# Linear attention followed by four Mamba scales: a tile of its own for inputs times step sizes, kept small weights, folded weights reloaded, attention weights for two passes

## The chip, the cores and the metric

The kernel runs on one core of one Trainium2 chip. The time is device microseconds of one execution; lower is better. The core has five engines with an instruction queue each: PE (matrix multiply, with its weight loads PEld), DVE (vector), ACT (activation functions), POOL (GpSimd) and SP, which here issues every DMA. Engines wait for each other by semaphores.

## What is computed

The input x has 8 samples of 512 channels and 48 x 48 = 2304 positions. Two layers follow each other; each adds its result to its input after a group norm:

```python
x = x + attention(gn(x))          # 8 heads of 64, causal, linear, feature elu+1
x = x + mamba4(gn(x))             # four scales of 128 channels, each fed by the one before

# one scale (b samples, L = 2304 positions, 128 channels in, 256 inside, 16 states)
xz = u @ Wi.T;  xp, z = split(xz, 2)
xs = silu(conv1d(xp, wc, 4 taps, depthwise, causal) + bc)
dt, Bm, Cm = split(xs @ Wx.T)                     # 8, 16, 16
delta = softplus(dt @ Wdt.T + bdt)
h_t = exp(delta_t * A) * h_(t-1) + (delta_t * xs_t) * B_t     # A = -exp(A_log)
y_t = (h_t . C_t) + xs_t * D
x_m = (y * silu(z)) @ Wo.T
fused = max(x_i, x_m)
out_i = sigmoid(mean(x_i)) * x_i + sigmoid(mean(fused)) * fused
x_(i+1) = split_(i+1) + out_i
```

All is float32.

## The kernel before

Positions are cut into 6 chunks of 384 columns. **Attention** works through 32 passes (8 samples x 4 tiles of 128 output channels), 6 chunks each: `chunk(m)`, lines 273 to 496. Its projections (L293) read the weights from `wq_sb`, which holds all 1536 output columns; `load_projections` (L106) loads the columns of one tile with three DMAs, and all four tiles are loaded in the start-up. In the first pass of a sample POOL also normalises the input xn (L317) and it is stored for the other three passes.

**Mamba** runs as two streams of four samples each. A stream takes a sample through its four scales; one sample and scale is a block, of six chunks. A chunk of a block is a job: 8 slots of two of the 16 states times two halves of the 256 channels, with four scans a slot. The 192 jobs of both streams alternate by a fixed list (`turns`, after four jobs of stream 0 alone). In each slot POOL and DVE form the products of B and delta times xs in `u` (L856, L867), ACT forms the decays in PSUM banks (L877), DVE runs the four scans (L888), POOL multiplies the result by C (L900), and PE sums it into `yp` (L916). `u` has five buffers, PSUM six banks.

**What orders the work.** The program is written out by hand: each slot has two halves, and preparations are tasks (generators) that stop at each `yield` with a time (in halves) and a number of banks; `beside` (L1056) advances those that are due. Each engine executes its instructions in the order in which the program writes them, SP its DMAs too. A task runs up to its first `yield` when it is made (L980).

**The parts that the change touches.**

- `Job.prepare` (L681) prepares one job: convolution (L693) and gate (L704) matmuls, silu, the projection to B, C and dt (L740), the step sizes delta = softplus (L764, into the one buffer of the tile delta), then `spread` (L771): delta is stored in a scratch in DRAM (L773, dscr) and read back spread over the partitions as dr. POOL multiplies delta by xs in place (L805), and the same tile is stored again (L773, xscr) and read back as dxr. Spreading is held to one job at a time by the list `spreading`.
- In the last job of a block, just ahead of the first `spread`, L769 makes the task `Stream.weights` (L510) for the stream's next block. It issues nine loads: in-projection wi, convolution wk (one row broadcast over the partitions), wo, wx, wd in two parts, pv in two parts, av. ACT then forms -exp of av (L536, L540), and POOL multiplies each of the four taps of wk by the projection (L539), so that the convolution becomes four matmuls on the raw input. `scaled` tells the next block's first job that wk is ready. This happens 32 times.
- `Stream.pass_on` (L561) ends a block and gives the stream its next input: ACT scales (L654, L655, L665), POOL adds (L662, L667, L670).
- `statistics(b)` (L216) forms the group norm of a sample for attention. For sample 0 it is the start-up: the six chunks of x, the weights of the first attention tile, the first xn, then the other tiles' weights.

## Time and profile before

| | |
|---|---|
| median of three runs | 8714.22 us (8709.94 to 8722.78) |
| the profiled execution | 8723.09 us |
| its span, first to last instruction | 8721.0 us |
| mean granted PE clock | 0.964 |
| DMA bytes of the program's own queue | 1635.13 MB |

| line | engine and work | count | mean ns |
|---|---|---|---|
| L888 | DVE scan | 6144 | 938 |
| L867 | DVE product | 1536 | 1195 |
| L900 | POOL weighing by C | 1536 | 3185 |
| L856 | POOL product | 1536 | 1283 |
| L805 | POOL delta times xs | 384 | 1005 |
| L539 | POOL folding of wk | 128 | 743 |
| L317 | POOL normalising xn | 192 | 673 |
| L877 | ACT decay | 6144 | 578 |

How to read it: a row of the profile names line, engine, operation and tiles (out<-in), how often it ran, its busy time and mean length, and the idle time of its engine just before it with what ended that idle time. Busy is not the same as on the path: only waits that delay the engine that is late at that place lengthen the run.

### The profile page before, as it was taken

The page shows a single profiled execution, that of the slowest core. Times are in us where ns is not written, and L with a number is a line of the kernel's source. Part 1 is how long each engine was busy: PE and PEld are TensorE (multiplying, and loading weights), DVE is VectorE, ACT ScalarE, POOL GpSimd, SP SyncE. Part 2 cuts the span into 40 slices and gives each one's busy share as a digit, 9 for nine tenths or more (in the row PEclk, how much of TensorE's full clock was granted, in tenths as well). Part 3 has the DMA queues.
Part 4 walks back from the last instruction along what each step waited for, and adds up shares of the span by engine and source line. Part 5 has one row for each costly group of instructions (what it writes and reads, how often), then busy time and mean ns, then how long its engine had stood idle before and what let it go on. Part 6 is the DMA issues. An engine that isn't in the chain of part 4 may idle for free. (4 is left out here: it accounts for less than half of the span.)

```text
span 8721.0 us, 124881 instructions
## 1 busy us (share of the span) xinstructions
PE 7774.7 (89%) x36482; PEld 3714.5 (43%) x36482; DVE 8072.2 (93%) x11078; ACT 6852.0 (79%) x14500; POOL 7834.3 (90%) x4343
## 2 busy tenths in 40 slices
PE   7899999988899999998889999999889999999965
PEld 4444444444444444444444444444444444444422
DVE  2899999999899999998899999999889999999998
ACT  2788888777788888877778888887777888888876
POOL 1789999999999999998998999998999889999998
PEclk9999999999999999999999999999999999999987
DMA  5667777776766777776676777776666667766665
GB/s 183 168 178 190 196 198 197 191 191 189 195 188 190 193 200 199 197 189 191 187 193 186 193 190 197 196 197 187 188 185 194 188 188 190 189 188 185 183 165 146
DMA packets 1002924, 1643.11 MB, mean 188 GB/s; under 512 B 138592, under 2 KB 797312, under 8 KB 1002240
## 3 DMA queue, kind: packets, MB, share of 16 engines
q1 hardware_dynamic: 1002240, 1635.13, 69.1%
q8 instruction: 290, 4.75, 0.2%
q14 instruction: 394, 3.23, 0.1%
HBM read 1309.06 MB, written 325.58 MB: 187 GB/s over the span
## 5 line engine op out<-in xcount | busy, mean ns | idle before, releaser
L888 DVE TENSOR_TENSOR_SCAN u<-bank,u 128x385 f32<-128x385 f32 (+1 forms) x6144 | 5455.4, 938 | 327.4 <-ACT bank L877 288.3
L900 POOL TENSOR_TENSOR u<-u,C 128x1536 f32<-128x1536 f32 x1536 | 4892.7, 3185 | 345.6 <-DVE u L888 186.9
L877 ACT ACTIVATE bank<-dr,av 128x385 f32<-128x385 f32 (+1 forms) x6144 | 3405.1, 578 | 671.0 <-DVE u L888 575.2
L916 PE MATMUL yp<-u,cst 128*64 128x384 f32 x12288 | 2417.7, 515 | 343.9 <-POOL u L900 259.6
L856 POOL TENSOR_TENSOR u<-B,dxr 128x512 f32<-128x512 f32 x1536 | 1969.9, 1283 | 17.5 <-DMA dxr<-xscr 15.4
L867 DVE TENSOR_TENSOR u<-B,dxp 128x1024 f32<-128x1024 f32 x1536 | 1835.0, 1195 | 9.7 <-ACT dxp L840 9.7
L293 PE MATMUL bank<-xn,wq_sb 128*128 128x384 f32 x4608 | 1725.8, 519 | 74.2 <-DVE u L888 33.0
L916 PEld LDWEIGHTS yp<-u,cst 128*64 128x64 f32 x12288 | 780.7, 139 | 1557.9 <-issue 871.9
L693 PE MATMUL bank<-xi,wk 128*128 128x384 f32 x3072 | 1110.7, 505 | 198.6 <-ACT kl L390 108.7
L293 PEld LDWEIGHTS bank<-xn,wq_sb 128*128 128x128 f32 x4608 | 867.4, 199 | 842.4 <-DVE u L888 140.0
L693 PEld LDWEIGHTS bank<-xi,wk 128*128 128x128 f32 x3072 | 558.8, 192 | 761.4 <-ACT kl L390 211.6
L805 POOL TENSOR_TENSOR delta<-delta,xs 128x384 f32<-128x384 f32 x384 | 385.7, 1005 | 361.8 <-DMA dscr<-delta 234.6
L305 ACT ACTIVATE ex<-bank,bqkv_sb 128x384 f32<-128x384 f32 x384 | 221.5, 577 | 505.3 <-PE bank L293 505.3
L877 ACT ACT_TABLE_LOAD x382 | 490.1, 1283 | 6.8
L845 ACT ACTIVATE yp<-xs,pv 128x384 f32<-128x384 f32 x384 | 223.6, 582 | 278.0 <-DVE yz L928 277.5
L934 PE MATMUL bank<-yz,wo 128*128 128x384 f32 x768 | 302.1, 510 | 24.4 <-DVE yz L928 17.3
L753 PE MATMUL bank<-dbc,wd 9*128 9x384 f32 x768 | 312.4, 527 | 3.7 <-ACT dbc L745 3.7
L704 PE MATMUL bank<-xi,wi 128*128 128x384 f32 x768 | 287.5, 495 | 9.7 <-ACT xs L729 9.7
L423 PE MATMUL bank<-cst,rdb 128*128 128x128 f32 x576 | 110.0, 304 | 200.9 <-DVE u L888 198.7
L740 PE MATMUL bank<-xs,wx 128*40 128x384 f32 x768 | 280.0, 487 | 2.7 <-ACT sm L457 2.7
L476 PE MATMUL bank<-sm,v 128*64 128x128 f32 x2304 | 257.1, 302 | 0.0
L729 ACT ACT_TABLE_LOAD x192 | 246.3, 1283 | 3.6 <-PE bank L693 0.2
(117 smaller groups left out, 7978.0 us busy)
## 6 DMA issues: line engine op xcount, KB each, us to landing
B<-scr SPq DMA_DIRECT2D x1536, 192.0 KB
C<-scr SPq DMA_DIRECT2D x1536, 192.0 KB
xn<-xn SPq DMA_DIRECT2D x192, 768.0 KB
dr<-dscr SPq DMA_DIRECT2D x768, 192.0 KB
dxr<-xscr SPq DMA_DIRECT2D x768, 192.0 KB
dscr<-delta SPq DMA_DIRECT2D x192, 384.0 KB
xscr<-delta SPq DMA_DIRECT2D x192, 384.0 KB
xn<-in_x SPq DMA_DIRECT2D x48, 768.0 KB
```

Of the source, the lines that this page charges most:

```text
L293: nc.tensor.matmul(ps, wq_sb[:, kt, j * 512 + o * P : j * 512 + (o + 1) * P], xn[:, kt, :], start=(kt == 0), stop=(kt == 3),)
L693: nc.tensor.matmul(xc, wk[:, k, h * P : (h + 1) * P], xi[:, c0 + k : c0 + k + LC], start=(k == 0), stop=(k == 3),)
L704: nc.tensor.matmul(zp, wi[:, 256 + h * P : 256 + (h + 1) * P], xi[:, c0 + 3 : c0 + 3 + LC], start=True, stop=True,)
L753: nc.tensor.matmul(vp, wd[32:41, h * P : (h + 1) * P], dbc[32:41, :], start=True, stop=True)
L805: nc.gpsimd.tensor_tensor(delta[:, h, :], delta[:, h, :], xs[:, h, :], ALU.mult)
L856: nc.gpsimd.tensor_tensor(u[:, :, :, 1 + LC - TAIL :], self.B[s % 4][:, :, cols].unsqueeze(2).to_broadcast(shape), self.dxr[s // 4][:, :, ...
L867: nc.vector.tensor_mul(u[:, :, :, 1 : 1 + LC - TAIL], self.B[s % 4][:, :, cols].unsqueeze(2).to_broadcast(shape), self.dxp.unsqueeze(1).to ...
L877: nc.scalar.activation(dA[:, cols], self.dr[h][:, g, cols], AF.Exp, scale=self.w[6][:, 2 * h + g, q + j : q + j + 1],)
L888: nc.vector.tensor_tensor_scan(u[:, j, g, cols], dA[:, cols], u[:, j, g, cols], 0.0, ALU.mult, ALU.add,)
L900: nc.gpsimd.tensor_tensor(u[:, :, :, 0:LC], u[:, :, :, 1:], self.C[s % 4].unsqueeze(2).to_broadcast([P, NG, 2, LC]), ALU.mult,)
L916: nc.tensor.matmul(self.yp[g * 64 : g * 64 + 64, 0:LC], pair_sum, u[:, j, g, 0:LC], start=False, stop=(s % 4 == 3 and j == NG - 1), skip_g ...
L934: nc.tensor.matmul(self.xm[:, 0:LC], self.w[2][:, h, :], self.yz[:, h, :], start=(h == 0), stop=(h == 1),)
```

## The change

There are four edits. (1) Delta times xs is written into a tile `dx` with one buffer; `spread` takes the tile to store. (2) Gate, out-projection, x-projection, bias, D and A of all four scales are packed into one array and loaded once into `scales`, step weights with their bias into `steps_w`; ACT forms -exp of A once for all scales, after the start-up's statistics. Uses index these tiles by the scale s. (3) `weights` loads only wk and, while a scale hasn't been folded, the projection wi: the folded wk is stored in DRAM once a scale, and later blocks of that scale, of either stream, load it back with one DMA. The list `folding` lets one stream fold at a time. (4) Attention weights are held for two passes: the tile wq of one pass (768 KB, packed on the host in one contiguous piece) has two buffers, and is loaded by one DMA in the fifth chunk of the pass before, right after that chunk has issued its fetch of the next xn.

```diff
-    wq_sb = cpool.tile([P, 4, 1536], F32, name="wq_sb")
-    def load_projections(o):
-        src = wqkv.rearrange("(t p) c -> p t c", p=P)
-        for j in range(3):
-            cols = slice(j * 512 + o * P, j * 512 + (o + 1) * P)
-            nc.sync.dma_start(out=wq_sb[:, :, cols], in_=src[:, :, cols])
+    wqs = []
+    def load_projections():
+        i = len(wqs)
+        if i < 4 * B:
+            o = parts[i * NC][1]
+            w = apool.tile([P, 4, 3 * P], F32, tag="wq", name=f"wq_{i}", bufs=2)
+            nc.sync.dma_start(out=w.rearrange("p t c -> p (t c)"), in_=wqkv[o])
+            wqs.append(w)
+    scales = cpool.tile([P, 4, 628], F32, name="scales")
+    steps_w = cpool.tile([64, 4, 256], F32, name="steps_w")
+    w_gate, w_out = scales[:, :, 0:256], scales[:, :, 256:512].rearrange("p s (h d) -> p s h d", h=2)
+    w_x = scales[:, :, 512:592].rearrange("p s (h d) -> p s h d", h=2)
+    w_cols = scales[:, :, 592:596]
+    w_a = scales[:, :, 596:628].rearrange("p s (h d) -> p s h d", h=4)
+    def load_scales():
+        nc.sync.dma_start(out=scales, in_=wall)
+        nc.sync.dma_start(out=steps_w[32:41], in_=wdt)
+        nc.scalar.activation(w_a, w_a, AF.Exp)
+        nc.scalar.mul(w_a, w_a, -1.0)
...
# chunk(m)
-                    wq_sb[:, kt, j * 512 + o * P : j * 512 + (o + 1) * P],
+                    wqs[m // NC][:, kt, j * P : (j + 1) * P],
...
         fetch(m + 1)
+        if c == NC - 2:
+            load_projections()
...
# Stream.weights: the nine loads, L536, L539 and L540 before; now
+            wk = wpool.tile([P, 4, 256], F32, tag=f"wk{z}", name=f"wk_{n}")
+            flat = wk.rearrange("p k d -> p (k d)")
+            self.coming = wk, s
+            if s in folded:
+                nc.sync.dma_start(out=flat, in_=folded[s])
+            else:
+                while folding:
+                    yield "1w", 0
+                folding.append(n)
+                wi = wpool.tile([P, 256], F32, tag="wi", name=f"wi_{n}")
+                nc.sync.dma_start(out=wi, in_=win[s])
+                nc.sync.dma_start(out=flat, in_=wconv[s].to_broadcast([P, 1024]))
+                for k in range(4):
+                    yield "3", 0
+                    nc.gpsimd.tensor_tensor(wk[:, k, :], wk[:, k, :], wi, ALU.mult)
+                folding.clear()
+                if s not in folded:
+                    folded[s] = dpool.tile([P, 1024], F32, tag="folded", name=f"folded_{s}")
+                    save(folded[s], flat)
             self.scaled = True
...
# Job.prepare
-            def spread(what):
-                s = dpool.tile([256, LC], F32, tag="dscr", name=f"{what}_{n}", bufs=6)
-                nc.sync.dma_start(out=s.rearrange("(h p) l -> p h l", h=2), in_=delta)
-                return s.rearrange("(h g d) l -> h d g l", h=2, g=2)
-            dsrc = spread("dscr")
+            def spread(what, of):
+                to = dpool.tile([256, LC], F32, tag="dscr", name=f"{what}_{n}", bufs=6)
+                nc.sync.dma_start(out=to.rearrange("(h p) l -> p h l", h=2), in_=of)
+                return to.rearrange("(h g d) l -> h d g l", h=2, g=2)
+            dsrc = spread("dscr", delta)
...
+            dx = mpool.tile([P, 2, LC], F32, tag="dx", name=f"dx_{n}", bufs=1)
             for h in range(2):
                 yield "1", 0
-                nc.gpsimd.tensor_tensor(delta[:, h, :], delta[:, h, :], xs[:, h, :], ALU.mult)
+                nc.gpsimd.tensor_tensor(dx[:, h, :], delta[:, h, :], xs[:, h, :], ALU.mult)
             yield "2", 0
-            xsrc = spread("xscr")
+            xsrc = spread("xscr", dx)
...
# start
         Task(statistics(0)).finish()
+        load_scales()
```

In `statistics(0)` the one remaining `load_projections()` loads the first pass's weights; the loop that loaded the other three tiles is gone. The other uses (gate, bias, x-projection, step weights, D, decay scale, out-projection) read the kept tiles in place of wi, pv, wx, wd, av and wo.

More of the change, by code (lines that the diff above doesn't have):

```diff
@@ L59, in attention_then_mamba_kernel @@
     wconv: bass.AP,
-    bconv: bass.AP,
-    wxp: bass.AP,
+    wall: bass.AP,
     wdt: bass.AP,
-    bdt: bass.AP,
-    alog: bass.AP,
-    dskip: bass.AP,
-    wout: bass.AP,
     out: bass.AP,
@@ L230, in statistics @@
                 load(c)
-            load_projections(0)
+            load_projections()
             for c in range(NC):
@@ L237, in statistics @@
                     fetch(0)
-            for o in range(1, 4):
-                load_projections(o)
         else:
@@ L340, in chunk @@
         fetch(m + 1)
+        if c == NC - 2:
+            load_projections()
         if o:
@@ L496, in chunk @@
             done[b, o] = norm
+    folded, folding = {}, []
     class Stream:
@@ L514, in weights @@
             self.scaled = False
-            wi = wpool.tile([P, 512], F32, tag=f"wi{z}", name=f"wi_{n}")
-            nc.sync.dma_start(out=wi, in_=win[s])
             wk = wpool.tile([P, 4, 256], F32, tag=f"wk{z}", name=f"wk_{n}")
-            nc.sync.dma_start(
-                out=wk.rearrange("p k d -> p (k d)"), in_=wconv[s].to_broadcast([P, 1024])
-            )
-            wo = wpool.tile([P, 2, P], F32, tag=f"wo{z}", name=f"wo_{n}", bufs=2)
-            nc.sync.dma_start(out=wo, in_=wout[s])
@@ L524, in weights @@
-            wx = wpool.tile([P, 2, 40], F32, tag=f"wx{z}", name=f"wx_{n}")
-            nc.sync.dma_start(out=wx, in_=wxp[s])
-            wd = wpool.tile([64, 256], F32, tag=f"wd{z}", name=f"wd_{n}")
-            nc.sync.dma_start(out=wd[32:40, :], in_=wdt[s])
-            nc.sync.dma_start(out=wd[40:41, :], in_=bdt[s])
-            pv = wpool.tile([P, 4], F32, tag=f"pv{z}", name=f"pv_{n}", bufs=2)
-            nc.sync.dma_start(out=pv[:, 0:2], in_=bconv[s])
-            nc.sync.dma_start(out=pv[:, 2:4], in_=dskip[s])
@@ L532, in weights @@
-            av = wpool.tile([P, 4, NS // 2], F32, tag=f"av{z}", name=f"av_{n}", bufs=2)
-            nc.sync.dma_start(out=av, in_=alog[s])
-            self.coming = wi, wk, wo, wx, wd, pv, av
-            yield "3", 0
-            nc.scalar.activation(av, av, AF.Exp)
-            for k in range(4):
-                yield "3", 0
-                nc.gpsimd.tensor_tensor(wk[:, k, :], wk[:, k, :], wi[:, 0:256], ALU.mult)
-            nc.scalar.mul(av, av, -1.0)
+            flat = wk.rearrange("p k d -> p (k d)")
@@ L684, in prepare @@
             n = self.n = f"{st.n}_{c}"
-            self.w = wi, wk, wo, wx, wd, pv, av = st.w
+            wk, s = self.w = st.w
             self.state, self.fsum, self.fm = st.state, st.fsum, st.fm
@@ L705, in gate @@
                     zp,
-                    wi[:, 256 + h * P : 256 + (h + 1) * P],
+                    w_gate[:, s, h * P : (h + 1) * P],
                     xi[:, c0 + 3 : c0 + 3 + LC],
@@ L728, in prepare @@
             ahead(DEPTH + 2)
-            nc.scalar.activation(xs[:, 0, :], xc0, AF.Silu, bias=pv[:, 0:1])
+            nc.scalar.activation(xs[:, 0, :], xc0, AF.Silu, bias=w_cols[:, s, 0:1])
             bank.free()
             zp1 = gate(1)
-            nc.scalar.activation(xs[:, 1, :], xc1, AF.Silu, bias=pv[:, 1:2])
+            nc.scalar.activation(xs[:, 1, :], xc1, AF.Silu, bias=w_cols[:, s, 1:2])
             nc.scalar.activation(sz[0], zp0, AF.Silu)
@@ L740, in prepare @@
                 nc.tensor.matmul(
-                    dps[0:40, 0:LC], wx[:, h, :], xs[:, h, :], start=(h == 0), stop=(h == 1)
+                    dps[0:40, 0:LC], w_x[:, s, h, :], xs[:, h, :], start=(h == 0), stop=(h == 1)
                 )
@@ L753, in prepare @@
                 nc.tensor.matmul(
-                    vp, wd[32:41, h * P : (h + 1) * P], dbc[32:41, :], start=True, stop=True
+                    vp, steps_w[32:41, s, h * P : (h + 1) * P], dbc[32:41, :], start=True, stop=True
                 )
@@ L845, in skip @@
             nc.scalar.activation(
-                yp[:, 0:LC], self.xs[:, h, :], AF.Copy, scale=self.w[5][:, 2 + h : 3 + h]
+                yp[:, 0:LC], self.xs[:, h, :], AF.Copy, scale=w_cols[:, self.w[1], 2 + h : 3 + h]
             )
@@ L880, in decay @@
                 AF.Exp,
-                scale=self.w[6][:, 2 * h + g, q + j : q + j + 1],
+                scale=w_a[:, self.w[1], 2 * h + g, q + j : q + j + 1],
             )
@@ L935, in project @@
                     self.xm[:, 0:LC],
-                    self.w[2][:, h, :],
+                    w_out[:, self.w[1], h, :],
                     self.yz[:, h, :],
@@ L1240 @@
     ]
+    win = np.swapaxes(np.asarray(L1_conv_in_proj_w), 1, 2)
+    packed = [
+        win[:, :, 256:512],
+        halves(np.swapaxes(np.asarray(L1_conv_out_proj_w), 1, 2)).reshape(4, P, 256),
+        halves(np.swapaxes(np.concatenate([wxp[:, bc_rows], wxp[:, :8]], axis=1), 1, 2)).reshape(4, P, 80),
+        halves(L1_conv_conv_b).reshape(4, P, 2),
+        halves(L1_conv_D).reshape(4, P, 2),
+        np.asarray(L1_conv_A_log)
+        .reshape(4, 4, 64, 8, 2)
+        .transpose(0, 4, 2, 1, 3)
+        .reshape(4, P, 32),
+    ]
     ins = {
@@ L1243 @@
         "consts": constants(),
-        "wqkv": lay(np.concatenate([wq, wkv], axis=0).T),
+        "wqkv": lay(
+            np.concatenate([wq, wkv], axis=0)
+            .reshape(3, 4, P, 4, P)
+            .transpose(1, 4, 3, 0, 2)
+            .reshape(4, P, 4 * 3 * P)
+        ),
         "bqkv": lay(np.concatenate([bq, bkv]).reshape(12, P).T),
-        "win": lay(np.swapaxes(np.asarray(L1_conv_in_proj_w), 1, 2)),
+        "win": lay(win[:, :, 0:256]),
         "wconv": lay(np.swapaxes(np.asarray(L1_conv_conv_w), 1, 2).reshape(4, 1, 1024)),
-        "bconv": halves(L1_conv_conv_b),
-        "wxp": halves(np.swapaxes(np.concatenate([wxp[:, bc_rows], wxp[:, :8]], axis=1), 1, 2)),
-        "wdt": lay(np.swapaxes(np.asarray(L1_conv_dt_proj_w), 1, 2)),
-        "bdt": lay(np.asarray(L1_conv_dt_proj_b).reshape(4, 1, 256)),
-        "alog": lay(
-            np.asarray(L1_conv_A_log).reshape(4, 4, 64, 8, 2).transpose(0, 4, 2, 1, 3).reshape(4, P, 4, 8)
-        ),
-        "dskip": halves(L1_conv_D),
-        "wout": halves(np.swapaxes(np.asarray(L1_conv_out_proj_w), 1, 2)),
+        "wall": lay(np.concatenate(packed, axis=2).transpose(1, 0, 2)),
+        "wdt": lay(
+            np.concatenate(
+                [
+                    np.swapaxes(np.asarray(L1_conv_dt_proj_w), 1, 2),
+                    np.asarray(L1_conv_dt_proj_b).reshape(4, 1, 256),
+                ],
+                axis=1,
+            ).transpose(1, 0, 2)
+        ),
     }
```

## The prediction

> **What bounds the kernel now.** I read the page first, then the list of waits, then the timeline through one block end, then busy time by stretch, and last the first 40 us. A job is one 384-column chunk of one Mamba stream: 8 slots of 4 scans; six jobs make a block (one sample and scale), and 192 jobs fill the span. The page:

> ```profile
> PE 7774.7 (89%) x36482; PEld 3714.5 (43%) x36482; DVE 8072.2 (93%) x11078; ACT 6852.0 (79%) x14500; POOL 7834.3 (90%) x4343
> ...
> L888 DVE TENSOR_TENSOR_SCAN u<-bank,u 128x385 f32<-128x385 f32 (+1 forms) x6144 | 5455.4, 938 | 327.4 <-ACT bank L877 288.3
> ...
> L805 POOL TENSOR_TENSOR delta<-delta,xs 128x384 f32<-128x384 f32 x384 | 385.7, 1005 | 361.8 <-DMA dscr<-delta 234.6
> ```

> DVE with its scans is the bound, idle for 649 us in all (8721 - 8072), some 170 of them in the start-up. POOL is close behind, and before the product L805 it stands idle for 361.8 us, mostly until the store of delta has landed, because L805 overwrites delta in place. The waits say how often, and that POOL's waits for broadcast loads are small:

> ```profile
> DVE u L888 <- ACT bank L877: 288.3, 213, 4.5
> ...
> POOL delta L805 <- DMA dscr<-delta: 234.6, 80, 24.4
> ...
> POOL u L900 <- DMA B<-scr: 31.6, 22, 2.1
> ```

> Is POOL's wait on the path? The timeline through a block end (start, length; SPq is SP issuing a DMA):

> ```profile
> 2632.66 0.87 ACT L764 ACTIVATE delta<-bank 128x384 f32<-128x384 f32 x2
> ...
> 2633.55 0.57 SPq L516 DMA_DIRECT2D wi<-in_win  x1
> ...
> 2638.46 1.29 POOL L856 TENSOR_TENSOR u<-B,dxr 128x512 f32<-128x512 f32 x1
> ...
> 2641.49 0.40 SPq L533 DMA_DIRECT2D av<-in_alog  x1
> ...
> 2642.83 0.38 SPq L773 DMA_DIRECT2D dscr<-delta  x1
> ...
> 2645.73 1.00 POOL L805 TENSOR_TENSOR delta<-delta,xs 128x384 f32<-128x384 f32 x1 [5.98 <-DMA dscr<-delta]
> ...
> 2646.70 3.18 POOL L900 TENSOR_TENSOR u<-u,C 128x1536 f32<-128x1536 f32 x1
> ...
> 2657.40 0.96 DVE L888 TENSOR_TENSOR_SCAN u<-bank,u 128x385 f32<-128x385 f32 x1 [2.60 <-ACT bank L877]
> ```

> ```profile
> 2656.19 0.71 ACT L665 ACTIVATE xi<-xb,norm_m 128x384 f32<-128x384 f32 x1 [5.37 <-POOL fu L662]
> ```

> Delta is ready at 2633.5, but SP first issues nine weight loads and reaches the store of delta 9.3 us later. The product starts 2.9 us after that. POOL, done at 2639.75, has stood for 5.98 us with the weighing L900 behind the product; some 11 us later DVE stands for 2.60 us. The last line (ACT alone, same place) shows the way there: ACT's next instruction waits 5.37 us for POOL's late add L662, and the decays for DVE stand behind it. Each of the 30 block ends looks so (stalls of 2 to 7.8 us, 181 us together). Outside them the stalls are mostly under 2 us, but for one of some 6.4 us two jobs after six of the block ends, and one of 24.4 us at the start.

> How much it hurts depends on POOL's other load. Two stretches of twelve jobs, busy us of PE, PEld, DVE, ACT, POOL, then clock, DMA share and GB/s:

> ```profile
> 1854.70:2412.10 557.40, 487.32 (x2267) 228.85 (x2267) 502.56 (x692) 429.55 (x911) 515.36 (x310) 0.96 0.71 191
> 2412.10:2931.50 519.40, 475.29 (x2285) 228.54 (x2284) 495.61 (x675) 429.83 (x911) 474.59 (x253) 0.99 0.70 190
> ```

> In the first POOL also normalises xn (L317) for the next sample's attention. There are three such stretches (557, 562 and 564 us). They hold only 7 us more DVE work than the second but last 38 to 45 us longer, and the PE clock falls: 0.50 from 6658 to 6664 us, after a block-end stall of 6.4 us that starved PE.

> [...]

> **The change, part by part.**

> *dx in its own tile.* The same 384 products at 1.00 us, so no work is added. What goes is the wait for the store of delta. The product now needs delta (softplus) and, as dx has one buffer, the previous job's store of dx, some 40 us back. Softplus of the next job needs the product as reader and the store of delta, both long done. SP's wait for the product before it issues the store of dx (L773) comes earlier. Nothing new is queued behind a wait.

> *Fewer weight loads.* Nine loads at each of 32 block starts (SP issue 0.24 to 0.57 us each, 8.3 us with waits in the timeline above) become one reload of 512 KB in 27 of them, and two loads in five (scale 0 for both streams, 1 to 3 for whichever comes first), plus four stores. As a task runs to its first stop when it is made, these still stand ahead of the store of delta; but that now costs one issue, about 0.5 us, and POOL no longer waits. POOL's folding falls from 128 multiplies of 743 ns (95 us) to 20 (15 us): 80 us less work, 3.0 us a block, hidden where POOL has slack, on the path in the three full stretches. ACT loses 62 instructions of 0.22 us (14 us), hidden. The strided weights are as wide as before for PE and ACT; I take 0, and at most 0.01 us for each of 6144 decays (60 us) if a strided scale cost anything.

> *Attention weights by pass.* 32 loads of 768 KB replace 12 of 256 KB, each issued about two chunks ahead, into a buffer whose last reader is five chunks back: no wait. Against the weights saved, traffic rises by about 11 MB of 1635 (0.7%) at a DMA share of 0.7. Each load lies ahead of later broadcasts for about 3.0 us (786 KB at 260 GB/s, what the busiest 3 us stretches moved). POOL waits only 31.6 us for B now, so I take 0; wholly exposed it would be 32 x 3.0 = 96 us.

> *Start-up.* The nine later loads of wq (10.4 us of SP) and 18 weight loads go; two packed loads (1.3 MB), one fold's loads and two ACT instructions come.

> ```profile
> 28.04 10.94 PE L293 MATMUL bank<-xn,wq_sb 128*128 128x384 f32 x24 [2.39 <-POOL xn L317]
> ...
> 34.21 0.23 ACT L536 ACTIVATE av<-av 128x32 f32<-128x32 f32 x1 [32.21 <-DMA av<-in_alog]
> ...
> 38.56 0.56 ACT L305 ACTIVATE ex<-bank,bqkv_sb 128x384 f32<-128x384 f32 x1
> ```

> ACT's first attention work waits behind av, whose data arrive at 34 and 38 us. The packed scales have about 2 MB less ahead of them, 7 to 8 us at 260 GB/s, and should land by about 28. The first exponential could then run when the first 8 of these 24 matmuls are done, by PE's weight loads at about 33, so 5 to 6 us earlier. PE is over 90% busy from 100 to 200 us, so that should last: -6 us, bounds 0 and -15. Stream 1's fold waits for stream 0's, but its first job is the fifth: 0.

> *The sum.* (a) Block ends: jobs that hold such a stall average 44.6 us outside the full stretches (first scan of one job to that of the next in the timeline), against 43.1 for the last three jobs of a block; the following one takes 0.3 more. 1.8 x 30 = 54, of which I expect 80% back: -43. The rest is kept by the reload, or by ACT. (b) The three full stretches last 114 us longer than three plain ones ((557 + 562 + 564) - 3 x 519 = 125, less 11 for a sample's norms on DVE, about as dear in other stretches). Without stalls and folding POOL needs about 515 - 12 = 503 us there, near DVE's 503, so I leave 11 us a stretch: 114 - 33 = -81. (c) Start: -6. Together -130. The profiled execution took 8723.1 (span 8721.0 and 2 around it): 8593. The median lies 9 lower: 8714 - 130 = 8584. DVE's idle 1.7 us in slot 7 of many jobs, while ACT loads tables and runs softplus, stays and is next.

> **Rivals.**

> *The stall moves.* POOL runs on, but DVE still waits for decays, as ACT was the one that ended its wait in the block end above. Speaks for it: 288 us of DVE's waits end with ACT, and ACT's own bursts don't change. Against it: there ACT itself waited for POOL. It would leave the start and a sixth of the rest: -6 - 21 = -27, 8687.

> *More comes back.* With slack, POOL no longer trails, [...]and the small stalls and half the 0.3 to 0.4 us idles in ordinary jobs go too: another 70 us, 8514. For it: six-job groups differ by more than their stalls. Against: ordinary stalls of 1 to 2 us show no DVE idle after them.

> *Slower: the attention weights hold up the broadcasts.* The load comes in the same step as an xn fetch of 768 KB, just ahead of the second half's dr and the last C. From 130 / 32 = 4.1 us of exposed delay a load, it eats the gain; 3.0 alone doesn't, [...]. Against: POOL's and ACT's waits for such loads hardly show now.

> **Chances.** The forecast's mechanism at about its size 0.72, more comes back 0.12, the stall moves 0.09, slower 0.07. A measurement of this kernel tells about 0.2% (17 us) from no change. Of the stall that moves, half is within it: faster 0.89, same 0.05, slower 0.06. The range goes from 8500 (a little beyond the second rival) to 8690 (a little beyond the first; 8584 with 60 us for the strided scale, or 96 for exposed loads, lies inside); it leaves out little but the slower case.

> **What would show it.** The product's idle falls from 362 us to under 60, and no wait of it names the store of delta; folding falls to 20 multiplies; the full stretches shrink to about 530 us with a clock of 0.98 or more; jobs at block ends go to about 43.3; the first exponential of attention runs near 33 us; POOL's waits for B and C stay under 60 us. If block ends keep their 2.6 us idle with POOL free, the first rival is right; if waits for dr, B or C appear after the attention loads, the third.

## The result, and the profile after

The changed kernel takes 8572.56 us (median of four runs, 8565.29 to 8572.92), the kernel before 8718.5 us (four runs, 8709.94 to 8729.34): a ratio of 0.9827, 95% interval 0.9815 to 0.9839, 146 us or 1.7% faster. The forecast was 8584, from the 8714 that was known of the kernel before. The profiled execution went from 8723.1 to 8565.3 us, its span from 8721.0 to 8563.5 and the mean PE clock from 0.964 to 0.973.

The page of the changed kernel; lines of before stand with the prediction (scan L888 is now L896, weighing L900 is L908, product L805 is L813):

```profile
PE 7704.4 (90%) x36482; PEld 3691.2 (43%) x36482; DVE 8067.9 (94%) x11078; ACT 6845.7 (80%) x14438; POOL 7758.3 (91%) x4235
...
L896 DVE TENSOR_TENSOR_SCAN u<-bank,u 128x385 f32<-128x385 f32 (+1 forms) x6144 | 5457.8, 940 | 254.2 <-ACT bank L885 253.8
L908 POOL TENSOR_TENSOR u<-u,C 128x1536 f32<-128x1536 f32 x1536 | 4889.0, 3183 | 606.8 <-DVE u L896 284.9
...
L813 POOL TENSOR_TENSOR dx<-delta,xs 128x384 f32<-128x384 f32 x384 | 385.5, 1004 | 22.3 <-ACT delta L771 22.3
```

The product's idle has fallen from 361.8 to 22.3 us, one wait in the start-up, and no store is named any more. POOL now stands mostly before the weighing, waiting for DVE: it has become the one that runs ahead. The scans' own idle fell from 327.4 to 254.2 us, and DVE's whole idle from 649 to 496 us (8563.5 - 8067.9): these 153 us are nearly all of the 157.5 us by which the span fell.

The waits (us in total, times, longest) show the path that the prediction drew, and the broadcasts that its third rival feared. First, three lines of the kernel before:

```profile
ACT xi L665 <- POOL fu L662: 88.0, 32, 7.7
...
DVE yz L928 <- PE yp L916: 41.0, 28, 5.8
...
DVE u L888 <- POOL u L856: 38.7, 34, 2.9
```

and the changed kernel:

```profile
DVE u L896 <- ACT bank L885: 253.8, 192, 3.8
...
POOL u L908 <- DMA B<-scr: 23.8, 14, 2.0
...
ACT xi L672 <- POOL fu L669: 21.9, 32, 1.5
POOL u L908 <- DMA C<-scr: 19.7, 11, 2.1
...
DVE yz L936 <- PE yp L924: 8.9, 5, 4.9
```

ACT's wait for POOL's late add fell from 88.0 us (longest 7.7) to 21.9 (longest 1.5). POOL's waits for B and C are 43.5 us together. The decays remain as DVE's wait, 192 times in 192 jobs. DVE's idle that ended with ACT's banks, over all lines, fell from 391 to 324 us. That is the predicted way, and it has less than half of the 153 us. DVE also waited for POOL's product u itself (38.7 us, now 0) and for PE's sum yp, which PE forms from POOL's weighed tiles (41.0 us, now 8.9); these two lines the prediction did not name.

A block end in the timeline (start, length):

```profile
2590.83 0.87 ACT L771 ACTIVATE delta<-bank 128x384 f32<-128x384 f32 x2
...
2592.91 0.54 SPq L533 DMA_DIRECT2D wk<-folded  x1
...
2593.53 0.61 SPq L780 DMA_DIRECT2D dscr<-delta  x1
...
2597.86 1.02 POOL L813 TENSOR_TENSOR dx<-delta,xs 128x384 f32<-128x384 f32 x1
...
2599.90 3.18 POOL L908 TENSOR_TENSOR u<-u,C 128x1536 f32<-128x1536 f32 x1 [1.02 <-issue]
```

One reload stands ahead of delta's store, which is issued 1.8 us after softplus and not 9.3; and the product, at its turn on POOL, starts without a wait.

Busy time of a full stretch and of the plain one after it (us of PE, PEld, DVE, ACT, POOL, then clock, DMA share, GB/s):

```profile
1842.90:2369.50 526.60, 476.39 (x2266) 225.80 (x2265) 504.14 (x691) 428.67 (x907) 507.14 (x299) 0.98 0.72 203
2369.50:2880.00 510.50, 467.84 (x2266) 225.58 (x2265) 492.39 (x671) 425.25 (x898) 467.91 (x244) 1.00 0.70 194
```

The full stretch shrank from 557 to 527 us and its clock rose from 0.96 to 0.98. DVE is busy for 96% of it.

To see where the time went, the jobs of each profiled execution were sorted by kind (a job's time is that from its first scan to that of the next): the 36 jobs of the three full stretches, and outside these the 24 jobs at block ends (those during which a block's last job is prepared and the next block's weights are loaded), the 24 after them, and 92 others. The first six and the last ten of the 192 jobs are left out. The column start is the time up to the first scan. The first line has us, the others differences to it. The kernels below the second line are the experiments of the next section; wq_alone and gap_filled_before, whose medians differ from before by nothing that can be told, show how far these sums scatter: up to 6 us.

| kernel | median us | ratio to before, 95% | start | full (36) | block ends (24) | next (24) | others (92) |
|---|---|---|---|---|---|---|---|
| before | 8718.5 | | 229.9 | 1683.7 | 1070.3 | 1041.9 | 3987.4 |
| changed | 8572.6 | 0.9827 (0.9815 to 0.9839) | -5.9 | -101.0 | -46.4 | -20.5 | +17.8 |
| store_first | 8637.9 | 0.9904 (0.9890 to 0.9917) | +2.7 | -38.3 | -44.8 | -20.6 | +20.0 |
| in_place | 8654.0 | 0.9925 (0.9911 to 0.9938) | -4.5 | -29.6 | -43.2 | -12.2 | +18.3 |
| in_place_pool_store | 8616.1 | 0.9881 (0.9864 to 0.9898) | -6.5 | -66.1 | -39.4 | -13.4 | +16.7 |
| wq_alone | 8716.3 | 0.9996 (0.9988 to 1.0004) | -5.0 | +6.2 | -4.2 | +4.0 | +1.2 |
| wq_and_own_tile | 8581.7 | 0.9839 (0.9825 to 0.9852) | -7.1 | -93.3 | -44.8 | -20.7 | +15.2 |
| fold_always | 8577.1 | 0.9840 (0.9826 to 0.9853) | -6.4 | -91.2 | -44.9 | -20.7 | +15.0 |
| weights_twice | 8572.7 | 0.9833 (0.9820 to 0.9847) | -6.3 | -99.6 | -46.6 | -20.7 | +18.3 |
| store_first_too | 8566.0 | 0.9828 (0.9814 to 0.9842) | -6.2 | -101.3 | -45.8 | -20.7 | +15.9 |
| gap_filled | 8553.0 | 0.9809 (0.9795 to 0.9824) | -3.3 | -97.5 | -44.0 | -20.7 | +0.1 |
| gap_half_filled | 8553.3 | 0.9810 (0.9793 to 0.9826) | -6.0 | -97.5 | -44.8 | -20.6 | +0.5 |
| gap_filled_before | 8723.7 | 1.0003 (0.9995 to 1.0011) | +2.1 | +1.0 | -1.0 | -1.5 | +2.2 |
| all_three | 8582.2 | 0.9838 (0.9824 to 0.9851) | -5.8 | -71.4 | -44.0 | -20.7 | +2.5 |

Two things in the second line ask for a cause: which of the four edits made the 101 us of the full stretches and the 67 of the plain block ends; and what made the other jobs 18 us slower, which no step of the prediction has.

### The profile page after: what moved, and what is told of

Its sections match the earlier page's. It is cut to its first block, busy times and chain, and to the rows that moved or that the text cites. A ratio compares the mean times of both kernels' runs of the same rounds, so it can differ in the third digit from the quotient of the medians.

```text
span 8563.5 us, 124248 instructions
## 1 busy us (share of the span) xinstructions
PE 7704.4 (90%) x36482; PEld 3691.2 (43%) x36482; DVE 8067.9 (94%) x11078; ACT 6845.7 (80%) x14438; POOL 7758.3 (91%) x4235
## 3 DMA queue, kind: packets, MB, share of 16 engines
q14 instruction: 388, 3.18, 0.1%
## 5 line engine op out<-in xcount | busy, mean ns | idle before, releaser
L896 DVE TENSOR_TENSOR_SCAN u<-bank,u 128x385 f32<-128x385 f32 (+1 forms) x6144 | 5457.8, 940 | 254.2 <-ACT bank L885 253.8
L908 POOL TENSOR_TENSOR u<-u,C 128x1536 f32<-128x1536 f32 x1536 | 4889.0, 3183 | 606.8 <-DVE u L896 284.9
L885 ACT ACTIVATE bank<-dr,scales 128x385 f32<-128x385 f32 (+1 forms) x6144 | 3412.3, 578 | 700.6 <-DVE u L896 598.1
L924 PE MATMUL yp<-u,cst 128*64 128x384 f32 x12288 | 2368.3, 506 | 176.5 <-POOL u L908 91.3
L303 PE MATMUL bank<-xn,wq 128*128 128x384 f32 x4608 | 1721.9, 518 | 66.3 <-DVE u L896 41.3
L303 PEld LDWEIGHTS bank<-xn,wq 128*128 128x128 f32 x4608 | 862.0, 197 | 837.9 <-DVE u L896 128.4
L853 ACT ACTIVATE yp<-xs,scales 128x384 f32<-128x384 f32 x384 | 223.4, 582 | 316.7 <-DVE yz L936 316.7
L813 POOL TENSOR_TENSOR dx<-delta,xs 128x384 f32<-128x384 f32 x384 | 385.5, 1004 | 22.3 <-ACT delta L771 22.3
L942 PE MATMUL bank<-yz,scales 128*128 128x384 f32 x768 | 303.2, 511 | 32.4 <-DVE yz L936 21.3
L760 PE MATMUL bank<-dbc,steps_w 9*128 9x384 f32 x768 | 301.2, 511 | 3.0 <-ACT dbc L752 3.0
L711 PE MATMUL bank<-xi,scales 128*128 128x384 f32 x768 | 288.6, 497 | 11.0 <-ACT xs L736 11.0
L747 PE MATMUL bank<-xs,scales 128*40 128x384 f32 x768 | 280.8, 488 | 2.7 <-ACT sm L469 2.7
```

The lines of the kernel that those rows point to most:

```text
L303: nc.tensor.matmul(ps, wqs[m // NC][:, kt, j * P : (j + 1) * P], xn[:, kt, :], start=(kt == 0), stop=(kt == 3),)
L711: nc.tensor.matmul(zp, w_gate[:, s, h * P : (h + 1) * P], xi[:, c0 + 3 : c0 + 3 + LC], start=True, stop=True,)
L760: nc.tensor.matmul(vp, steps_w[32:41, s, h * P : (h + 1) * P], dbc[32:41, :], start=True, stop=True)
L813: nc.gpsimd.tensor_tensor(dx[:, h, :], delta[:, h, :], xs[:, h, :], ALU.mult)
L885: nc.scalar.activation(dA[:, cols], self.dr[h][:, g, cols], AF.Exp, scale=w_a[:, self.w[1], 2 * h + g, q + j : q + j + 1],)
L896: nc.vector.tensor_tensor_scan(u[:, j, g, cols], dA[:, cols], u[:, j, g, cols], 0.0, ALU.mult, ALU.add,)
```

## The experiments

**Which part does it: the nine loads, or the own tile?** The theory at the start (A) was that the loads ahead of the store were the cause, so that moving the store, or having fewer loads, would bring most of the gain.

store_first, the kernel before with one line moved:

```diff
+            dsrc = spread("dscr")
             if c == NC - 1 and (st.s < 3 or st.samples):
                 tasks.append(Task(st.weights()))
...
-            dsrc = spread("dscr")
```

> The kernel before, with one line moved: delta's store is issued ahead of the task that loads the next block's weights. Theory A (the nine loads ahead of the store on SP made the stall): the store goes out at once, the product's idle falls from 362 us to about 150, the block-end jobs and the ones after them give back most of their 67 us and the full stretches about 50 of their 101 (the folding stays), so 8718 - 110 = 8610 us, between 8590 and 8640. Theory B (any wait of the product for a store in its own place costs as much): product still idle over 250 us, time 8690 or more.

in_place, the changed kernel without its first edit:

```diff
-                nc.gpsimd.tensor_tensor(dx[:, h, :], delta[:, h, :], xs[:, h, :], ALU.mult)
+                nc.gpsimd.tensor_tensor(delta[:, h, :], delta[:, h, :], xs[:, h, :], ALU.mult)
...
-            xsrc = spread("xscr", dx)
+            xsrc = spread("xscr", delta)
```

> The changed kernel, with the product put back in delta's own tile. Theory A: one reload stands ahead of the store, so the product waits 2 to 4 us at the block ends and 1 to 2 us elsewhere, which POOL's slack covers: 8573 + 10, between 8565 and 8600 us, so the own tile itself brings little once the loads are few. Theory B (the own tile is what brought the 130 us): over 8640 us.

Measured: 8637.9, at the edge of what A expected, and 8654.0, which is B's (over 8640) and not A's. So A doesn't hold for the kernel as a whole. The table says where: at the plain block ends either cure brings nearly all (-44.8 and -43.2 of -46.4), but in the full stretches only 38 and 30 of 101. Before the product POOL stands idle for 212 us in store_first, and not the 150 that A expected; in in_place it stands as long as in the kernel before:

```profile
L806 POOL TENSOR_TENSOR delta<-delta,xs 128x384 f32<-128x384 f32 x384 | 385.0, 1003 | 211.9 <-DMA dscr<-delta 95.5
...
L812 POOL TENSOR_TENSOR delta<-delta,xs 128x384 f32<-128x384 f32 x384 | 384.3, 1001 | 362.9 <-DMA dscr<-delta 261.4
```

Before, the second row had 361.8 us of idle and the kernel took 65 us more. The sum of a wait doesn't tell its cost. By kind of job, in_place's idle is 65 us at plain block ends, 38 in the jobs after them, 130 in others and 99 in the full stretches (141, 2, 84 and 106 before). Outside the full stretches it now comes in pieces of 5 us or less, and all the jobs there take only 12 us more than in the changed kernel: POOL's slack swallows most of it. In the full stretches POOL has little slack, and pieces of up to 6.5 us remain; these jobs take 71 us more.

wq_alone and wq_and_own_tile separate the two other edits: the kernel before with edit 4 alone, and with edits 4 and 1, so that the difference of the two is the own tile's. Nine loads and 128 foldings stay in both.

```diff
# wq_alone, its matmuls (the loads as in the changed kernel)
...
-                    wq_sb[:, kt, j * 512 + o * P : j * 512 + (o + 1) * P],
+                    wqs[m // NC][:, kt, j * P : (j + 1) * P],
...
# wq_and_own_tile, besides
...
-                nc.gpsimd.tensor_tensor(delta[:, h, :], delta[:, h, :], xs[:, h, :], ALU.mult)
+                nc.gpsimd.tensor_tensor(dx[:, h, :], delta[:, h, :], xs[:, h, :], ALU.mult)
...
```

> The kernel before, with the attention weights loaded by pass and nothing else. My step took 0 for the exposed loads and -3 for the shorter start: 8715, between 8700 and 8730 us. The rival (loads hold up the broadcasts, 3 to 6 us each) gives 8815 to 8910.

> The kernel before, with the attention weights by pass (which frees the room) and dx in a tile of its own; the nine loads and the 128 folding multiplies stay. Theory A and the prediction's first step: the product's idle under 80 us, block ends as in the changed kernel (-67), full stretches half-way (-50): 8718 - 117 = 8600 us, between 8580 and 8640. Rival (the late store of delta now delays dr, or ACT's wait stays): 8670 or more. Rival (the folding is what cost): 8690.

Measured: 8716.3, no difference that can be told, and 8581.7. In the second the product waits once, in the start-up:

```profile
L809 POOL TENSOR_TENSOR dx<-delta,xs 128x384 f32<-128x384 f32 x384 | 386.8, 1007 | 22.4 <-ACT delta L767 22.4
```

The own tile alone brings 135 us (8716.3 - 8581.7) with all nine loads still ahead of the store; that's nine tenths of the change. The half-way guess for the full stretches (-50) was too small, they gave 93. What edits 2 and 3 add to it is 9 us between the two medians: the intervals of the two ratios overlap, the single runs (8574.4 to 8585.1 against 8565.3 to 8572.9) don't.

**What makes the full stretches different.** The timeline of store_first in the first full stretch, around a stall in which POOL waits for itself:

```profile
1898.39 1.11 SPq L798 DMA_DIRECT2D C<-scr  x2
...
1903.71 0.87 ACT L764 ACTIVATE delta<-bank 128x384 f32<-128x384 f32 x2
...
1908.30 0.69 POOL L317 TENSOR_SCALAR xn<-xn,norm_a 128x384 f32<-128x384 f32 x1
...
1909.02 0.38 SPq L167 DMA_DIRECT2D xn<-xn  x1
...
1911.54 0.58 SPq L268 DMA_DIRECT2D xn<-in_x  x1
...
1913.43 0.53 SPq L770 DMA_DIRECT2D dscr<-delta  x1
...
1920.83 1.00 POOL L806 TENSOR_TENSOR delta<-delta,xs 128x384 f32<-128x384 f32 x1 [6.25 <-DMA xr<-in_x]
```

Delta is ready at 1904.6. SP has issued nothing since 1899.5: it stands at the store of xn until POOL has normalised the last quarter (ends 1909.0), then issues what is queued, and reaches delta's store at 1913.4, just behind the load of the next xn (768 KB). The product runs at 1920.8, after 6.25 us of POOL's idle. (The wait is put down to the DMA that ended last; the product itself needs the store of delta.) To test this circle, the xn store in the kernel of in_place was given to POOL, which has just made the data:

```diff
-            save(xns[b].rearrange("(t p) l -> p t l", p=P)[:, :, cols], xn)
+            nc.gpsimd.dma_start(out=xns[b].rearrange("(t p) l -> p t l", p=P)[:, :, cols], in_=xn)
```

> The kernel of the run in_place (product in delta's own tile, few loads), but the store of the normalised xn is issued by POOL, which has just made it, and no longer by SP, which stood there until POOL was done. POOL gains 48 issues. Theory D (in the full stretches SP stands at the xn store for POOL's normalising while delta's store is behind it, so POOL waits for itself): the stalls of 6.4 us at the product in these stretches go, and the time falls from 8654 to 8610, between 8590 and 8630 us. Rival (the store's own latency, or the xn load ahead of it, makes the stall): 8645 or more.

Measured: 8616.1, 38 us less than in_place, and all of it in the full stretches (-66 for -30). There the product's idle fell from 99 to 4 us:

```profile
L812 POOL TENSOR_TENSOR delta<-delta,xs 128x384 f32<-128x384 f32 x384 | 383.8, 1000 | 272.9 <-DMA dscr<-delta 231.5
```

So theory D holds, and has 37 of the 71 us that in_place lacks in the full stretches. The issues cost POOL time too: 36 of the 48 lie in the full stretches, at 0.81 us each (the last experiment has them in the changed kernel). What else keeps this kernel from -101 wasn't taken apart.

**Is the folding worth anything, and do the attention weights cost?**

```diff
# fold_always
-            if s in folded:
-                nc.sync.dma_start(out=flat, in_=folded[s])
-            else:
+            if True:
# weights_twice
             wqs.append(w)
+            w = apool.tile([P, 4, 3 * P], F32, tag="wq2", name=f"wq2_{i}")
+            nc.sync.dma_start(out=w.rearrange("p t c -> p (t c)"), in_=wqkv[o])
```

> The changed kernel, with the convolution weights folded at every block (128 multiplies of 743 ns and two loads) in place of the reload of a folded copy: 80 us more work for POOL. Prediction's step: hidden where POOL has slack, on the path in the three full stretches (six blocks, 3 us each): 8573 + 20, between 8580 and 8600 us. Rival (hidden throughout): within 5 us of 8573. Rival (all of it on the path): 8650.

> The changed kernel, with each attention weight load of 768 KB made twice, the second copy into a tile that nothing reads: 25 MB more. Prediction's step (the load is hidden): within 10 us of 8573. Rival (each load holds up the broadcasts behind it for 3 to 6 us): 8573 + 96 to 192.

Measured: 8577.1 and 8572.7. In fold_always POOL does 94.2 us of folding (128 at 737 ns) where the changed kernel does 14.5 (20); of these 80 us, 10 show in the full stretches, where these sums scatter by up to 6, and some 5 in its median, where the intervals of the ratios overlap. The median is within 5 us of 8573, as the first rival expected, and below the 8580 of the prediction's step: nearly all of the folding is hidden. In weights_twice the traffic rises from 1646 to 1672 MB and the time not at all. Together with wq_alone this shows that the load of 768 KB is hidden whole, and the prediction's third rival has nothing to stand on.

**Is anything left of the store's order?**

```diff
# store_first_too: store_first's move, in the changed kernel
+            dsrc = spread("dscr", delta)
             if c == NC - 1 and (st.s < 3 or st.samples):
```

> The changed kernel, with delta's store issued ahead of the weight task as well. Theory A: what the loads cost is already gone (one issue of 0.54 us stands ahead, and no one waits for the store for long): within 10 us of 8573. Rival (the product's neighbours still wait for dr behind the reload): 8550 or less.

Measured: 8566.0 (8564.88 to 8575.77), no difference that can be told. With the own tile and one reload, where delta's store stands doesn't matter.

**The 18 us that the other jobs lost.** They sit in the third job of a block (14, 20, 26, 104 and on): 45.4 us where it was 44.1, with DVE idle for 2.1 to 3.0 us in the last slot where it was 0.5 to 1.7. ACT waits there for a convolution, that of the job two places ahead (16, 22, 28 and on, the first of the other stream's next block), and this convolution runs slowly. Busy time by stretch for PE alone (length, busy us and count, clock, DMA share, GB/s), in the changed kernel and then in the kernel before, each cut at the steps of its own clock:

```profile
871.09:874.51 3.42, 1.48 (x8) 1.00 0.36 102
874.51:877.92 3.41, 3.41 (x8) 0.50 0.30 105
877.92:881.33 3.41, 3.41 (x18) 1.00 0.94 217
```

```profile
877.08:880.49 3.41, 2.96 (x14) 1.00 0.84 192
880.49:883.91 3.42, 1.94 (x6) 1.00 0.29 88
883.91:887.32 3.41, 3.17 (x18) 1.00 0.56 166
```

The same gap of 1.93 us (PE waits for POOL's xi) stands in both. In the changed kernel it falls whole into one window, whose busy share is then 0.43, and the next window is at half clock (0.50). In the kernel before, a window's edge divides it, the shares are 0.87 and 0.57, and the clock stays at 1.00. (A window is one step of 3.413 us: in the traces of these two kernels all changes of the clock, 187 and 237, lie on one grid of this step.) In the trace of the changed kernel 97 of 140 windows under half busy are followed by one at half clock, and 36 of 2367 of the others. Of these 36, 27 were at half clock already, so that the clock didn't fall but stayed low: all 19 windows at half clock with a busy share from 0.50 to 0.78 were followed by another.

Of the 20 plain jobs that have this gap, 11 have the slow convolution in the changed kernel, none in the kernel before, 12 in store_first and 9 in in_place. The 11 gaps begin 0.04 to 0.14 of a window after an edge; the 9 others of the changed kernel begin within 0.04 of an edge or 0.46 to 0.65 after it, and all 20 of the kernel before 0.48 to 0.89. The eleven jobs take 13 us longer than in the kernel before, of the 18. It seems to keep itself going: with the loss a block lasts 259.5 us, 76.0 windows, so that the next block's gap falls into nearly the same place, and five such jobs in a row (152 to 176) have it. Theory C, then: the 18 us come from these gaps that lie whole in one window, and with such a gap filled the convolution behind it runs at full clock.

gap_filled puts two matmuls that nobody reads into the gap, gap_half_filled one, gap_filled_before two into the kernel before (there with wi and cst as operands):

```diff
             def conv(h):
                 xc = bank()[:, 0:LC]
+                if h == 0 and self.start // SLOTS % 6 == 4:
+                    for _ in range(2):
+                        nc.tensor.matmul(
+                            xc, w_gate[:, s, 0:P], scales[:, 0, 0:LC], start=True, stop=True
+                        )
```

> The changed kernel, with two matmuls that nobody reads put into PE's idle 1.93 us ahead of the first half of the convolution, in one job of each six. Theory C (the +18 us of ordinary jobs is PE's clock: [...]eleven of these gaps fall whole into one window in the changed kernel, none in the kernel before): no such job runs at half clock, the second half of its convolution starts 5.2 us after the first and not 6.57, DVE's idle in those slots falls from 2.6 to 1.2 us, time 8573 - 11 x 1.4 = 8557, between 8545 and 8565 us. Rival (ACT's chain sets it anyway, or the blocks fall elsewhere into the windows): within 5 us of 8573. Rival (the two matmuls are in the way): 8573 + 20.

> As gap_filled, with one matmul of 128x384 in place of two: PE's idle in the gap falls from 1.93 to about 1.55 us and its busy share of a window that holds the whole gap rises from 0.43 to 0.54. Theory C with a threshold at half: as good as two matmuls, 8553, between 8545 and 8562 us. Rival (the threshold is higher, about 0.6): 8566 to 8580, jobs still at half clock.

> The kernel before, with the same two matmuls that nobody reads in the same gap of PE, in one job of each six. Theory C: in the kernel before, none of these gaps falls whole into one window of PE's clock, so there is nothing to win: within 8 us of 8719. Rival (filling the gap helps whatever the windows): 8700 or less. Rival (the matmuls are in the way): over 8730.

Measured: 8553.0, 8553.3 and 8723.7, all as theory C has it. The runs of gap_filled (8542.7 to 8557.8) don't overlap those of the changed kernel (8565.3 to 8572.9). The first half of the convolution behind the gap in the timeline (in brackets PE's idle before it), in the changed kernel and in gap_half_filled:

```profile
873.37 4.41 PE L700 MATMUL bank<-xi,wk 128*128 128x384 f32 x8 [1.94 <-POOL xi L674]
```

```profile
873.49 2.85 PE L705 MATMUL bank<-xi,wk 128*128 128x384 f32 x8 [1.10 <-POOL xi L674]
```

In the profiles of these three kernels none of the 20 jobs has the slow convolution, and the other jobs' +18 is gone in the first two. In these two DVE's idle in the last slot of the eleven jobs is 0.5 to 1.7 us again. One matmul filled 0.84 us of the gap and not the 0.4 that was expected (the four matmuls of the rows above are eight instructions), so it raised the share to 0.43 + 0.84 / 3.41 = 0.68. Half clock came after a share of 0.43 and not after 0.68, so the run can't tell a step at half from one at 0.6. Of the windows at full clock in all 14 traces, 155 of 319 with a busy share from 0.40 to 0.46 were followed by half clock, 545 of 759 from 0.46 to 0.50, and 16 of 1187 from 0.50 to 0.58; above that it was 37 of 2159 in the trace of the kernel before and 8 of 2153 in that of the changed kernel. These shares come from modelled ends of matmuls.

**All together.** The one matmul, store_first's move and POOL's store of xn, in the changed kernel (each edit as above):

> The changed kernel with the one matmul in PE's gap, the xn store issued by POOL, and delta's store ahead of the weight task. If the own tile has already taken the product out of every wait for a store, the last two bring nothing more: 8553, between 8544 and 8562 us. Rival (dr and the broadcasts behind SP's standing still cost in the full stretches): 8540 or less. Rival (POOL's 48 issues cost): 8565 or more.

Measured: 8582.2, 29 us more than gap_half_filled, 26 of it in the full stretches. The last rival holds. As store_first_too cost nothing in the changed kernel, POOL's stores are what is left; no run has them alone with the own tile. The issues, by line:

```profile
L335 POOL DMA_DIRECT2D xn<-xn x48 | 38.9, 810 | 14.9 <-POOL xn L327 14.9
```

36 of them lie in the full stretches, and with them POOL is busy 30 us longer there. Of the 26 us, DVE's idle has 7; 17 are longer DVE instructions, of which this is one (timeline):

```profile
1898.21 3.18 POOL L914 TENSOR_TENSOR u<-u,C 128x1536 f32<-128x1536 f32 x1
...
1898.94 4.66 DVE L590 TENSOR_SCALAR wt<-wt 128x2 f32<-128x2 f32 x1
1901.36 0.99 POOL L819 TENSOR_TENSOR dx<-delta,xs 128x384 f32<-128x384 f32 x1
1902.31 1.26 POOL L870 TENSOR_TENSOR u<-B,dxr 128x512 f32<-128x512 f32 x1
```

A DVE instruction on two numbers a row took 4.66 us (median of this line: 0.16) and ended 0.03 us after POOL's third instruction, in POOL's first pause. It was not the only one: every instruction of L590, and of the norm's products, that took over 0.6 us in this profile and in those of the two kernels compared, ended 0.01 to 0.04 us after the end of a POOL instruction. In the full stretches the small scalings of this tile (the busy time of DVE's tensor-scalar instructions on wt) take 1 us in the kernel before, in store_first and in in_place, 17 in the changed kernel, and about 28 in the two kernels in which POOL issues the stores. So it seems (the author's reading; no run tests it) that a POOL without pauses gives back a little of what it won.

The fastest kernel here is gap_filled, or gap_half_filled: 8553, 1.9% below the kernel before.

## Why the prediction was right

The mechanism was the predicted one: POOL's wait for the store of delta was on DVE's path, mostly in the full stretches, and it is gone. The time lies 11 us below the forecast; that it lies so near is in part luck, as the terms below were off by more, in both directions. Against the profiled executions the sum was -130 and came to -158; 12 us less show in the medians, as the profiled execution of before lay some 5 us above its median and that of the changed kernel 7 below.

- **The wait for the store, step (a).** Right: gone, and with it most of ACT's wait for POOL. The size was too small: the 24 block ends outside the full stretches and the jobs after them were to bring 43 x 24 / 30 = 34 us together; the first brought 46 and the second 20. The mis-sized term is the measure of an undisturbed job: 43.1 us, the last three of a block. Without the wait, jobs at block ends and after them take 42.7 and 42.6. Nor was a fifth kept by the reload or ACT. The own tile alone brings nearly all of it, with the nine loads still in place (66 us in wq_and_own_tile), and so does the moved store alone (65 us in store_first).
- **Full stretches, step (b).** With (a)'s share of their six block ends the forecast was -81 - 9 = -90; measured -101. They last 528 us on average (530 expected), the clock is 0.98. But the sum laid the gain on two things, stalls and folding, and put 12 us a stretch on the folding. A stretch has two blocks, and its trace 8 folding multiplies or 5.9 us; fold_always shows some 3 (10 / 3). The rest is stalls. A good part of these came from SP standing at xn's store (in_place_pool_store), which the prediction listed as stalls of 6.4 us two jobs after a block end without a cause.
- **Start, step (c).** -6 expected, -5.9 measured; the first exponential of attention ran at 31.96 us (33 expected), ACT's wait for the scales ended at 25.45. Kernels with the old start gave 229.9 to 232.6 and those with the new one 222.8 to 226.6, so the size holds to about 3 us. wq_alone, with edit 4 and without edits 2 and 3, already has 5.0 of it.
- **Costs taken as zero.** Attention weights: zero, by wq_alone and weights_twice. Strided scales: zero, a decay takes 578 ns before and after. One reload ahead of the store: zero, by store_first_too. Traffic rose by 11 MB, as worked out.
- **What no step had.** The +18 us of PE's clock. It hides in the sum because (a) and (b) were sized too small: 33 and 11 us too little there, 18 too much here. The prediction named a clock of 0.50 from 6658 us, after a stall that starved PE. There the clock fell at 6655.8, after a window in which PE was still busy for 0.63 of 3.41 us: so the trace of before already had half clock behind a window that wasn't idle.
- **The rivals.** The stall didn't move: DVE's waits for decays fell by 34.5 us (288.3 to 253.8). More did come back than forecast, but not by that rival's way: ordinary jobs got slower. The third had no place, since POOL's waits for B and C came to 43.5 us (under 60 expected); the 6 us a load in the expectations was the author's estimate, twice the 3.0 us worked out from 260 GB/s, and no run shows it. What was named as next, DVE's idle in the last slot, is still there.

## What to carry over

Here POOL overwrote in place a tile that was being stored, and its wait held more than the store (2.9 us from issue to product): also what stood ahead of the store in SP's queue, at a block end of the kernel before nine loads (9.3 us), in a full stretch SP's own wait for POOL (9.5 us, from 1899.5 to 1909.0 in store_first). In such a kernel try a tile of its own for the second result before you shorten the queue: here the one brought 135 us, the other 65. Size a gain by where a wait lies (has the waiting engine slack there?), since 363 us of it cost 81 us in one kernel (in_place), and 362 us cost 135 in another (the kernel before); and after such a change look at PE's clock in jobs that the edit doesn't touch (18 us here).
